# Layer 2's weights times the adjacency, on GpSimd and in the adjacency's own tile

## The chip, the cores and the metric

The kernel runs on one core of a Trainium2 chip. A core has five engines with instruction queues of their own: TensorE (PE in the profile; PEld are its weight loads), VectorE (DVE), ScalarE (ACT), GpSimd (POOL) and SyncE (SP), which issues the DMAs here. Each engine works through its queue in order; semaphores order the engines among each other. The metric is the device time of one execution in microseconds (us). Lower is better.

## The reference

Four layers over a batch of 32 graphs, each with 512 nodes, 64 features and a weighted 512x512 adjacency. Each layer adds its result to x and normalises.

```python
x = layernorm(x + L0(x, adj))            # (adj / clip(deg, 1)) @ x
x = layernorm(x + L1(x, adj, W, b))      # Chebyshev polynomials of the Laplacian, k = 4
x = layernorm(x + L2(x, adj, attW, attb))
x = layernorm(x + L3(x, adj, mask, W1, b1, W2, b2))

# layer 2
x_local = logmap(x[:, :, None, :], x[:, None, :, :], c)    # all pairs i, j
logits  = concat([x_self, x_local]) @ att_W + att_b
att     = sigmoid(logits) * adj
support = einsum('bij,bijd->bid', att, x_local)
out     = proj(expmap(clip(support), x, c), c)

# layer 3: neighbours are the places with adj > 0 without the diagonal; where a node has
# more than 10, some are removed; then a weighted sum of the 0.25, 0.5 and 0.75 quantiles
# of the neighbours' features goes through a two-layer perceptron
```

The change touches layer 2's product with `adj`, and what layer 3 reads of `adj`.

## The kernel before

All work of all 32 graphs is written down first and issued afterwards. Each helper (`tt`, `ts`, `stt`, `act`, `mm`, `tr`, `gtt`, `gts`) calls `Order.op` with the engine, a planned issue time, a planned tail, a closure, and the tiles that it writes and reads. `Order.op` finds the dependencies in program order: read after write, write after read, and the turn of a tile's buffers. `Order.issue` then simulates the five engines with the planned times, picks on each the ready operation with the earliest due time, and issues all of them in that order, pinned on each engine. A due time is 80 us times the graph's number plus a place in its lane's stage (`STAGES`, L1420). On PE it puts filler matmuls (L1458) into planned idle time. The planned cost of a DVE `tt` on two f32 tiles in SBUF is 0.07 us + 1.04 ns per element.

The lanes of a graph, in the order in which they are written down:

- `front` (due -0.6 to -0.5): four column blocks of the adjacency are loaded into `A`, transposed on PE and copied by ACT into `AT` (L780), a tile of [128, 4, 512] f32 with two buffers. Layers 0 and 1 multiply by it. The result goes into `FL`.
- `pairs` (due 1.2 to 1.3): layer 2 over all pairs of nodes, with tiles of one buffer each (`FT`, `EX`, `RW`, `Q`, `L`, `Wt`). `Q` holds a factor of the logarithmic map for each pair; its upper blocks come from a `tt` on DVE (L1066), the lower ones from transposes of these and an ACT copy. `L` is the sigmoid of the logits, made from a matmul in PSUM times `Q` (L1076). Then `Q` is multiplied by `AT` (L1080), `L` is transposed and multiplied by this product into `Wt` (L1086), and `Wt` goes through matmuls with `FL`.
- `tail` (due 0.2 to 1.5): the rest of layer 2, many small [128, 4] operations on POOL and wider ones on DVE; it ends with `x3` and `x3h`.
- `graph` (due 0.9 to 1.0): layer 3's neighbours. `nbT` is the comparison `AT > 0` on DVE (L787), with the diagonal taken out. From it come degrees, the removed edges `v`, the mask `V`, the order of nodes by degree, `perm`, `VP` and `slot`.
- `gather` (2.7 to 2.9): one-hot tiles `oh` from `slot` on DVE, matmuls with `x3h`, ACT copies into `SB` and `SH`.
- `sort` and `head` (4.5 to 5.6): sorting networks of `tt` minima and maxima on DVE over `SB` and `SH`, products with tables, layer 3's perceptron and the output.

The lanes of several graphs are interleaved on every engine. In the profile a tile's name has its lane in front: `pairs_Q`, `front_AT`, `graph_nbT`. Lines are often those of a helper: L448 is `tt`, L452 `ts`, L455 `stt`, L471 `gtt`, L475 `gts`, L483 `act`, L502 `mm`, L507 `tr`, L719 the power on POOL in `rsqrt`.

In program order, `pairs` of a graph is written down before its `graph`. Before the change `graph` and the product of L1080 only read `AT`, so they wait for nothing of each other.

Of the kernel before, what the change touches and what calls it, by code (L numbers as in the profile page):

```python
# [15 lines left out]
OP = mybir.AluOpType  # L16
# [387 lines left out]
def tile_adj_resnorm(ctx: ExitStack, tc: tile.TileContext, x, adj, nodemask, w1k, b1k, att_w, att_b,  # L404
                     w1, b1, w2, b2, out):
    nc = tc.nc
    B, N, D = x.shape
    T = N // P
# [16 lines left out]
    seq = Order(nc, tc)  # L425
# [7 lines left out]
    def vec(f, out, ins, one=False, scalars=(), reads=None, **kw):  # L433

        n = width(reads if reads is not None else out)
        tiles = [out] + list(ins)
        rate = 1.04e-3
        if not any(a.space == PSUM for a in tiles):
            half = all(a.dtype in (F16, BF16) for a in tiles)
            if one:  # L440
                rate = 0.26e-3 if half else 0.52e-3
            elif half:
                rate = 0.52e-3
        sc = [a for a in scalars if isinstance(a, bass.AP)]
        seq.op("DVE", 0.07 + n * rate + 0.065 * len(sc), 0.085, f, [out], list(ins) + sc)

    def tt(out, a, b, op):
        vec(lambda: nc.vector.tensor_tensor(out, a, b, op=op), out, [a, b])  # L448
# [5 lines left out]
    def stt(out, a, s, b, op0, op1):  # L454
        vec(lambda: nc.vector.scalar_tensor_tensor(out, a, s, b, op0=op0, op1=op1), out, [a, b], False, (s,))  # L455
# [21 lines left out]
    def act(out, a, f, bias=None, scale=1.0, accum_out=None, after=None):  # L477
        sc = [x for x in (bias, scale) if isinstance(x, bass.AP)]
        kw = {k: v for k, v in (("bias", bias), ("accum_out", accum_out)) if v is not None}
        n = width(out)  # L480
        table = "exp" if f in (AF.Ln, AF.Exp) else "sig" if f in (AF.Sigmoid, AF.Tanh) else None
        seq.op("ACT", 0.12 + n * 0.83e-3 + 0.09 * len(sc) + (0.2 if accum_out is not None else 0.0),
             0.3, lambda: nc.scalar.activation(out, a, f, scale=scale, **kw), [out, accum_out], [a, after] + sc, table)  # L483
# [22 lines left out]
    def tr(out, a, ident):  # L506
        seq.op("PE", 0.115 if a.dtype == F32 else 0.058, 0.6, lambda: nc.tensor.transpose(out, a, ident), [out], [a, ident],  # L507
               (128, 64 if width(a) <= 64 else 128))
# [6 lines left out]
    def bank(dtype=F32, home=None):  # L515
        lane, seq.lane = seq.lane, home or seq.lane
        t = seq.tile(pools["ps"], [P, 512 if dtype == F32 else 1024], dtype, "bank", bufs=BANKS.get(seq.lane, 2))
        seq.lane = lane
        return t
# [219 lines left out]
    def rowsum(a, b, name):  # L739

        pr = wide("pr")
        tt(pr, a, b, op=OP.mult)
        s = col(name)
        reduce(s, pr, OP.add)
        return s
# [223 lines left out]
    def pairs(b, res):  # L969

        mid = pools["mid"]
        AT, FL = res["AT"], res["FL"]
# [3 lines left out]
        pt = bank()  # L976
# [51 lines left out]
        pt = bank()  # L1028
# [9 lines left out]
        for j in range(T):  # L1038
            n = N - j * P
            o = slice(OB[j], OB[j + 1])  # L1040
            pt = bank()
            mm(pt[:, :n], FT[:D + 3, 2, j * P:(j + 1) * P], FT[:D + 3, 0, j * P:], start=True, stop=True)
            act(E[:, o], pt[:, :n], AF.Relu)
            pt = bank()
# [16 lines left out]
        Q = seq.tile(mid, [P, T, N], F32, "Q", 1)  # L1061
        for o in parts2:
            tt(W[:, o], W[:, o], X[:, o], op=OP.subtract)
        for j in range(T):
            o = slice(OB[j], OB[j + 1])
            tt(Q[:, j, j * P:], R[:, o], W[:, o], op=OP.mult)  # L1066
            if j:
                pt = bank()
# [4 lines left out]
        for i in range(T):  # L1073
            pt = bank()
            mm(pt, FT[:D + 3, 1, i * P:(i + 1) * P], FT[:D + 3, 2, :], start=True, stop=True)
            stt(L[:, i, :], pt, 0.5, Q[:, i, :], op0=OP.mult, op1=OP.mult)  # L1076
            act(L[:, i, :], L[:, i, :], AF.Sigmoid, bias=oo[:, i:i + 1])
        for g in range(2):
            gs = slice(2 * g, 2 * g + 2)
            tt(Q[:, gs, :], Q[:, gs, :], AT[:, gs, :], op=OP.mult)  # L1080
        Wt = seq.tile(mid, [P, T, N], F32, "Wt", 1, "RW")
        for j in range(T):
            pt = bank()
            for i in range(T):
                tr(pt[:, i * P:(i + 1) * P], L[:, i, j * P:(j + 1) * P], identf)
            stt(Wt[:, j, :], pt, 0.5, Q[:, j, :], op0=OP.mult, op1=OP.mult)  # L1086
        pt = bank()[:, :T * (D + 2)].rearrange("p (t n) -> p t n", n=D + 2)
        for t in range(T):
            for j in range(T):
# [8 lines left out]
        q = rowsum(x2, S, "xs")  # L1098
# [325 lines left out]
    with ExitStack() as fast:  # L1424
# [42 lines left out]
        for b in range(B):  # L1467
            if b % 2 == 0:
                both = {"ends": []}
            res = dict(both)  # L1470
            seq.batch = b
            for lane, f in (("front", front), ("pairs", pairs), ("graph", stage_graph), ("gather", gather), ("sort", sort)):
                seq.lane = lane
                f(b, res)
            both["ends"].append((res["slots"][1], res["x3"][0]))
            both.update(ohm=res["ohm"], ap=res["ap"])
            if b == B - 1:
                both["spots"] = spots(both["ends"])
            if b % 2:
                seq.lane = "head"  # L1480
                head(b, both)
# [144 lines left out]
    with tc.If(flagv > 0):  # L1626
        with ExitStack() as slow:
# [31 lines left out]
            for h in range(2):  # L1659
                f = cst.tile([P, D], F32, name=f"fold{h}")  # L1660
                g = cst.tile([P, D], F32, name="foldg")
# [48 lines left out]
```

## Time and profile before

| what | us |
|---|---|
| median of three runs (lowest to highest) | 2580.22 (2572.68 to 2582.51) |
| the profiled execution's own time | 2575.55 |
| its span, from the first to the last instruction | 2573.7 |
| DVE busy, of the span | 2382.1 |
| PE busy, of which L1458's filler matmuls 141.5 | 2413.6 |
| ACT busy | 1837.6 |
| POOL busy | 848.9 |
| DVE: the product of `Q` and `AT`, 64 of [128, 1024] | 78.2 |
| DVE: the comparison into `nbT`, 32 of [128, 2048] | 38.9 |

Busy time is the union of an engine's instructions; "mean ns" of a row is the length of one record, and neighbouring records of DVE overlap at their ends. The granted TensorE clock was 0.979 over the span. The four busiest rows of DVE are the two sorting networks (SB 566.8 us, SH 341.6 us), the one-hots (257.0 us) and a product of layer 2 (103.6 us). POOL's largest rows are the powers of `rsqrt` on [128, 4], some 1.2 to 1.3 us each; its products on [128, 4] have a mean of 0.25 to 0.5 us.

### The profile page before, as it was taken

Reading aid. Unit: us, or ns where it says so; the run is one execution under the profiler, and the core shown is the slowest. Engines: PE = TensorE matmul, PEld = TensorE weight load, DVE = VectorE, ACT = ScalarE, POOL = GpSimd, SP = SyncE. Lnnn points to the kernel's source line nnn. Section 1 sums busy time; section 2 is a strip of 40 time slices with the busy share of each in tenths; the row PEclk is TensorE's granted clock in tenths of the full one; section 3 lists DMA queues with packets and bytes.
Section 4 is the critical chain, followed back from the end, with each engine's and each line's share of the span. In section 5 each row is a group of like instructions: output and inputs, shape, how many; then the busy total and the mean of one; then the engine's idle time right before and its main releaser. Section 6 shows DMA issues by size and latency. Waiting matters only on the chain.

```text
span 2573.7 us, 56084 instructions
## 1 busy us (share of the span) xinstructions
PE 2413.6 (94%) x19895; PEld 1635.0 (64%) x19918; DVE 2382.1 (93%) x8937; ACT 1837.6 (71%) x4156; POOL 848.9 (33%) x2007
## 2 busy tenths in 40 slices
PE   7999989999999999999999999999999999999997
PEld 6766666656666666666666666666666666666555
DVE  4669999999999999999999999999999999999996
ACT  5766677777677777777677776877777777777761
POOL 1234434333234333323343433333333333333210
PEclk9999999999899999999999999998999999999998
DMA  1100000000000000000000000000000000000000
GB/s 39 36 22 21 22 14 13 24 22 26 20 15 19 16 26 22 24 10 22 22 20 26 22 22 22 12 22 20 26 22 18 16 18 24 20 12 3 8 5 8
DMA packets 119723, 49.98 MB, mean 19 GB/s; under 512 B 53740, under 2 KB 119436, under 8 KB 119436
## 3 DMA queue, kind: packets, MB, share of 16 engines
q1 hardware_dynamic: 118272, 46.15, 6.5%
q8 instruction: 158, 2.59, 0.4%
q14 instruction: 129, 1.06, 0.1%
q10 hardware_dynamic: 1164, 0.18, 0.0%
HBM read 37.93 MB, written 8.39 MB: 18 GB/s over the span
## 4 chain that ended last, share of the span: by engine, by line
DVE 73%; PE 20%; ACT 4%; issue 2%; POOL 1%; DMA 0%; ACTq 0%; DVEq 0%
DVE SB L448 17%; DVE SH L448 10%; DVE gather_oh L452 7%; PE pairs_bank L502 4%; DVE pairs_Q L448 4%; PE front_bank L502 4%; PE graph_bank L502 3%; PE gather_bank L502 3%; DVE pairs_RW L448 3%; DVE sort_prod L448 3%; DVE pairs_Wt L455 3%; DVE pairs_L L455 2%; PE head_bank L502 2%; DVE pairs_RW L455 2%; DVE pairs_EX L448 1%
## 5 line engine op out<-in xcount | busy, mean ns | idle before, releaser
L448 DVE TENSOR_TENSOR SB<-SB 128x92 f32<-128x92 f32 (+11 forms) x1424 | 566.8, 425 | 12.6
L502 PE MATMUL gather_bank<-gather_oh,tail_x3h 128*64 128x448 f16 (+5 forms) x5376 | 522.0, 319 | 5.6 <-ACT SB L483 4.2
L502 PEld LDWEIGHTS <-tail_x3h 128*64 128x64 bf16 x5376 | 294.7, 110 | 201.8 <-issue 95.7
L448 DVE TENSOR_TENSOR SH<-SH 128x128 f32<-128x128 f32 (+10 forms) x1744 | 341.6, 247 | 7.8
L502 PE MATMUL pairs_bank<-pairs_FT 67*128 67x512 f32 (+7 forms) x768 | 323.0, 522 | 16.6 <-DVE pairs_EX L455 9.4
L452 DVE TENSOR_SCALAR gather_oh<-graph_slot 128x256 f16<-128x256 f16 (+9 forms) x864 | 257.0, 337 | 19.1 <-PE gather_bank L502 17.0
L502 PE MATMUL front_bank<-front_AT,front_y 128*64 128x256 f32 x1536 | 193.5, 387 | 16.5 <-DVE front_y L448 15.5
L502 PEld LDWEIGHTS pairs_bank<-pairs_FT 67*128 67x128 f32 (+1 forms) x768 | 132.3, 196 | 85.3 <-issue 22.7
L502 PEld LDWEIGHTS front_bank<-front_AT,front_y 128*64 128x64 f32 x1536 | 118.1, 138 | 72.7 <-DVE front_y L448 18.9
L502 PE MATMUL graph_bank<-graph_perm,graph_V 128*128 128x512 f16 x512 | 141.6, 384 | 17.4 <-DVE graph_perm L452 16.0
L502 PEld LDWEIGHTS <-graph_nbT 128*128 128x128 f16 x1536 | 113.2, 99 | 57.7 <-issue 15.3
L1458 PE MATMUL PA<-zero 128*128 128x256 bf16 x1022 | 141.5, 280 | 0.1
L502 PEld LDWEIGHTS front_bank<-XA,front_AT 128*128 128x128 f32 x1024 | 126.2, 192 | 15.7 <-issue 6.6
L471 POOL TENSOR_TENSOR tail_nr<-tail_nr,tail_y 128x4 f32<-128x4 f32 x96 | 37.1, 386 | 285.6 <-DVE tail_y L461 230.4
L719 POOL TENSOR_TENSOR front_rs<-front_var,mhalf 128x4 f32<-128x4 f32 x64 | 81.5, 1273 | 145.7 <-DVE front_var L452 130.1
L502 PE MATMUL pairs_bank<-FLS,pairs_Wt 128*128 128x66 f32 x1024 | 123.8, 275 | 2.7 <-DVE pairs_Wt L455 2.2
L502 PEld LDWEIGHTS pairs_bank<-FLS,pairs_Wt 128*128 128x128 f32 x1024 | 119.4, 192 | 9.1 <-DVE pairs_Wt L455 7.1
L502 PE MATMUL front_bank<-XA,front_AT 128*128 128x65 f32 x1024 | 124.4, 272 | 0.3 <-ACT front_AT L483 0.3
L502 PEld LDWEIGHTS <-tabs 128*128 128x128 f16 x1296 | 78.6, 98 | 62.4 <-issue 49.6
L448 DVE TENSOR_TENSOR pairs_RW<-pairs_RW,pairs_EX 128x640 f32<-128x640 f32 x128 | 103.6, 816 | 13.7 <-ACT pairs_RW L483 9.2
L1458 PEld LDWEIGHTS <-zero 128*128 128x128 bf16 x1022 | 98.9, 101 | 23.8 <-issue 8.5
L483 ACT ACTIVATE SB<-gather_bank 128x448 f32<-128x448 f32 (+2 forms) x192 | 80.9, 439 | 45.0 <-PE gather_bank L502 44.2
(355 smaller groups left out, 6451.8 us busy)
## 6 DMA issues: line engine op xcount, KB each, us to landing
front_A<-in_adj_dram SPq DMA_DIRECT2D x128, 256.0 KB, 2.7
XA<-in_x_dram SPq DMA_DIRECT2D x32, 128.0 KB, 2.3
xs<-tail_x SPq DMA_DIRECT2D x32, 128.0 KB, 1.9
out_dram<-head_zo SPq DMA_DIRECT2D x31, 128.0 KB, 2.0
out_dram<-tail_ends SPq DMA_DIRECT2D x1, 128.0 KB, 2.1
wk<-in_L_gnn_weight_dram ACTq DMA_DIRECT2D x1, 64.0 KB, 3.1
w1s<-in_L_gnn_W_dram ACTq DMA_DIRECT2D x2, 32.0 KB, 1.9
attw<-in_L_gnn_att_W_dram ACTq DMA_DIRECT2D x2, 0.2 KB, 3.5
```

Of the source, the lines that this page charges most:

```text
L448: vec(lambda: nc.vector.tensor_tensor(out, a, b, op=op), out, [a, b])
L452: vec(lambda: nc.vector.tensor_scalar(out, a, s1, s2, op0=op0, **kw), out, [a], True, (s1, s2))
L455: vec(lambda: nc.vector.scalar_tensor_tensor(out, a, s, b, op0=op0, op1=op1), out, [a, b], False, (s,))
L471: gp(lambda: nc.gpsimd.tensor_tensor(out, a, b, op=op), out, [a, b])
L483: 0.3, lambda: nc.scalar.activation(out, a, f, scale=scale, **kw), [out, accum_out], [a, after] + sc, table)
L502: return nc.tensor.matmul(out, w, a, start=start, stop=stop)
L719: seq.op("POOL", 0.8, 0.6, lambda: nc.gpsimd.tensor_tensor(y, v, mhalf, op=OP.pow), [y], [v])
L1458: return nc.tensor.matmul(PA[:, 2 * P:], zero[:, :P], zero, start=False, stop=False)
```

## The change

The two DVE products of 1024 elements per partition become four POOL products of 512 elements, one for each row block. Each multiplies a row block of `AT` by the row block of `Q` and writes the result over that row block of `AT`. `Wt` is made from `AT` in place of `Q`. The planner is told 1.2 us for a product and a tail of 0.5 us.

```diff
-        for g in range(2):
-            gs = slice(2 * g, 2 * g + 2)
-            tt(Q[:, gs, :], Q[:, gs, :], AT[:, gs, :], op=OP.mult)
+        for j in range(T):
+            a = AT[:, j, :]
+            seq.op("POOL", 1.2, 0.5, lambda a=a, q=Q[:, j, :]: nc.gpsimd.tensor_tensor(a, a, q, op=OP.mult), [a], [a, Q[:, j, :]])
         Wt = seq.tile(mid, [P, T, N], F32, "Wt", 1, "RW")
         for j in range(T):
             pt = bank()
             for i in range(T):
                 tr(pt[:, i * P:(i + 1) * P], L[:, i, j * P:(j + 1) * P], identf)
-            stt(Wt[:, j, :], pt, 0.5, Q[:, j, :], op0=OP.mult, op1=OP.mult)
+            stt(Wt[:, j, :], pt, 0.5, AT[:, j, :], op0=OP.mult, op1=OP.mult)
```

Three relations change with it. The product no longer writes `Q`, so it does not wait until the four `L` have read `Q`. `AT` is written in `pairs`, so `graph`'s comparison, which comes later in program order, now waits for the product and reads it in place of the adjacency; off the diagonal the factor in `Q` is positive, so the comparison with zero means the same. And `AT` is read until the last `Wt` is made.

## The prediction

> **What bounds the kernel now.** I read the page's first lines, then the slices and the chain of waits.
>
> ```profile
> PE 2413.6 (94%) x19895; PEld 1635.0 (64%) x19918; DVE 2382.1 (93%) x8937; ACT 1837.6 (71%) x4156; POOL 848.9 (33%) x2007
> ...
> DVE  4669999999999999999999999999999999999996
> ...
> DVE 73%; PE 20%; ACT 4%; issue 2%; POOL 1%; DMA 0%; ACTq 0%; DVEq 0%
> ```
>
> After a start of about 190 us DVE is full to the last slice, and the chain that ended last runs over it for 73% of the span. PE looks as busy, but 141.5 us of it are the fillers of L1458, which are issued only into planned idle time; its own work is 2413.6 - 141.5 = 2272.1 us. A table of stretches gives the steady state exactly (columns: PE, PEld, DVE, ACT, POOL busy).
>
> ```profile
> core 0: us, PE busy (x) PEld busy (x) DVE busy (x) ACT busy (x) POOL busy (x), PEclk, DMA share, GB/s
> ...
> 600.00:1200.00 600.00, 570.38 (x4685) 383.34 (x4690) 577.88 (x2172) 450.32 (x1024) 199.29 (x475) 0.98 0.08 21
> 1200.00:1800.00 600.00, 569.47 (x4680) 382.63 (x4684) 576.40 (x2155) 441.44 (x1009) 210.24 (x478) 0.98 0.07 20
> 1800.00:2400.00 600.00, 567.39 (x4664) 378.44 (x4669) 581.46 (x2179) 449.96 (x1020) 212.63 (x479) 0.99 0.06 17
> ```
>
> DVE is busy 96 to 97% there. So a microsecond of DVE time given back or lost on each graph moves the end by about as much; POOL has two thirds of its time free.
>
> **What is removed.** The view of the tile Q shows the product that goes, and its two neighbours on DVE.
>
> ```profile
> L455 DVE SCALAR_TENSOR_TENSOR pairs_L<-pairs_bank,pairs_Q x128: 651/681/693, 104.0 to 2422.3; 128x512 f32<-128x512 f32 x128
> L455 DVE SCALAR_TENSOR_TENSOR pairs_Wt<-pairs_bank,pairs_Q x128: 658/680/692, 111.9 to 2430.0; 128x512 f32<-128x512 f32 x128
> L448 DVE TENSOR_TENSOR pairs_Q<-pairs_Q,front_AT x64: 1203/1224/1261, 105.6 to 2423.2; 128x1024 f32<-128x1024 f32 x64
> ```
>
> Sixty-four products of 1.224 us each (shortest, median, longest in ns). Records of DVE overlap by some 80 ns: where another follows at once, the next starts 1.14 us after. Gain: 64 x 1.14 = 73 us of DVE. The stt that makes Wt keeps its size and only reads AT in place of Q: nothing changes in its 0.68 us.
>
> **What is added.** 128 products of 128x512 f32 on POOL. No POOL instruction of the trace reads more than 8 elements per partition; its widest that write are in the start-up:
>
> ```profile
> 1.03 0.53 POOL L539 MEMSET UC<- 128x512 f16 x1
> ...
> 1.65 0.56 POOL L547 IOTA ii<- 128x512 int32 x1
> 2.16 0.14 POOL L550 IOTA ic<- 128x4 int32 x1
> ```
>
> From 4 to 512 elements iota grows by 0.42 us, 0.83 ns per element, for one stream written. A 128x4 product takes 0.20 us undisturbed. With one, two or three such streams one after the other a 128x512 product takes 0.62, 1.04 or 1.46 us. I take 1.04: two operands read, the write beside them. POOL gains 128 x 1.04 = 133 us, from 849 to 982 of some 2,600: no bound in itself.
>
> **What it does to DVE** decides the sign. One window has both cases, POOL first, DVE second:
>
> ```profile
> 1589.07 0.20 POOL L471 TENSOR_TENSOR pairs_sq<-FLS 128x4 f32<-128x4 f32 x1
> 1589.23 0.20 POOL L475 TENSOR_SCALAR pairs_two<-FLS 128x4 f32<-128x4 f32 x1
> 1589.52 1.13 POOL L471 TENSOR_TENSOR pairs_al<-pairs_two,FLS 128x4 f32<-128x4 f32 x1
> ```
>
> ```profile
> 1588.70 0.68 DVE L455 SCALAR_TENSOR_TENSOR pairs_L<-pairs_bank,pairs_Q 128x512 f32<-128x512 f32 x1
> 1589.30 0.16 DVE L452 TENSOR_SCALAR FLS<-FLS 128x8 f32<-128x8 f32 x1
> 1589.37 1.21 DVE L448 TENSOR_TENSOR pairs_Q<-pairs_Q,front_AT 128x1024 f32<-128x1024 f32 x1
> ```
>
> Under pairs_L, with one operand in PSUM, a POOL instruction of four elements takes 0.20 us. Under the product with two operands in SBUF, such an instruction takes 1.13 us and ends when that product ends. This is regular. I took all small POOL instructions that begin with over 250 ns of a DVE instruction still to go: under SB<-SB 128x448 all 92 were held until about 0.14 us after its end, under gather_oh 128x1792 all 26, under pairs_L none of 45, under pairs_Wt none of 22. So one engine at a time has the way to SBUF, for a whole DVE instruction. The reverse is not in the trace: POOL's own accesses are too short, and DVE's SB 128x448 takes 620 ns beside POOL work and 617 without it. Bounds of what a POOL product costs DVE: nothing, if DVE goes first and POOL gets the gaps; or its whole 0.62 to 1.46 us, if POOL holds as DVE does. I take that it holds, the nearest row being DVE's own holding, and POOL streams all the while.
>
> Not every DVE instruction wants the way then. Adding up DVE from 200 to 2400 us, each until the next starts, instructions with two SBUF operands or a tensor_scalar in SBUF take 1677 of 2122 us (79%); in the 15 us after the last tt into Q, where the new products fall, 10.3 of 15 us (69%). I take 75%. Cost: 128 x 1.04 x 0.75 = 100 us of DVE, with 0.62 and 1.46 as ends 60 and 140. Net on DVE: -73 + 100 = +27, from -13 to +67.
>
> The Trainium skill, "SBUF — State Buffer", section "Who interferes with whom", speaks against this change. It says that a DVE instruction with two SBUF inputs and a GpSimd one that reads SBUF exclude each other, and that whichever is issued second is blocked fully until the first is done. The trace agrees for POOL as second, with the 1.13 us above; no run here shows DVE as second. By the rule the net is the +27 just worked out, by the rows alone it could also be the -73.
>
> **What is moved.** Three things wait longer. (1) The product now lies in AT, and the graph lane's comparison (L787) reads AT later in program order, so it waits for POOL.
>
> ```profile
> L452 DVE TENSOR_SCALAR graph_nbT<-front_AT x32: 1193/1218/1229, 29.0 to 2390.3; 128x2048 f16<-128x2048 f32 x32
> ```
>
> It ran 22 to 33 us ahead of the product (batch 31: 2390.3 against 2423.2). From it to the batch's last slot copy passed 57 us in batch 0, 86 in batch 20, 74 in batch 31. Batch 20: slot would be done at 1593 + 4 + 86 = 1683 in place of 1636, 21 us after x3h (1662), which gather's matmuls need too. What hides these 21 us is the wait of sort: the last one-hot of batch 20 was made at 1722, its sorted sum was out at 1833, 111 us for a lane with 566.8/32 = 18 us of DVE work on SB. The cover ends with the run: slot(31) goes from 2465 to 2424 + 4 + 57 to 74 = 2485 to 2502, against x3h(31) at 2492, 0 to +10; I take +8, near the 74 of the same stretch. (2) AT's two buffers come free at the last Wt, in batch 20 at 1599.2, not at the product's end, 1592.8, after which the copies into AT of batch 22 began at 1593.5: 6.4 us later. The cover is the time that FL is ready before FT is copied, mostly 15 to 25 us (batch 22: 1662 to 1688). If it were gone, half of 6.4 us per graph, 102 us. I take 0. (3) Small POOL operations queue behind the products: those of tail, front's rsqrt, head's. Up to 4 x 1.04 = 4.2 us per graph; POOL is 1% of the chain, and DVE has other lanes' work meanwhile; 0, at worst 133 us in all. Wt waits for the products itself, but from the last tt into Q to the last sigmoid are some 19 us (batch 20: 1574 to 1593), against 4.2 us. No DMA is added or removed; loads into A wait, if at all, with the copies of (2).
>
> The order is laid out anew with 1.2 us for each product and 2.3 us less DVE per graph. DVE's idle share of 3 to 4% may change by a point either way: 22 us in 2,200.
>
> **Sum.** The profiled execution took 2575.6 us (span 2573.7 and 1.9 around it). 2575.6 - 73 + 100 + 8 = 2610.6. The median of the runs lies 4.6 higher, at 2580.2: 2615.
>
> **Rivals.**
> (B) DVE goes first, and POOL works in its gaps and under its PSUM instructions: 2580 - 73 + 8 = 2515, 2505 to 2545 as the order falls. For it: POOL waited through several DVE instructions on end (3.58 us from 1341.9). Against it: usually it got in after the one instruction it met. PE would not stop it: its 2272 us are below DVE's 2309. This is the case on the other side: it decides from where a POOL product costs DVE less than 73/128 = 0.57 us, or, with the 8 us, 0.51.
> (C) The hand-over of AT or POOL's queue gets on the path besides: with half of the 102 us, 2666; for it: in batches 3 and 15 FL was ready only 6 us ahead. Against it: the mean cover is twice what is added.
> (D) Gain and blocking cancel, products falling under pairs_L and pairs_Wt, which let POOL through (2.4 us each per graph): 128 x 1.04 x 0.5 = 67, so 2582.
>
> **How the numbers follow.** Forecast (A) 0.60, B 0.20, C 0.14, D 0.06. The time is A's, 2615; A's own range, with a hold of 0.62 to 1.46 us and part of the order's 22 us, is 2565 to 2665. With C's lower half and B's upper half: 2525 to 2672. Half a per cent, 13 us, is what a measurement can tell from no change: 2567 to 2593. Faster: B 0.19 and 0.03 of A, 0.22. Same: D 0.06, 0.01 of B, 0.11 of A, 0.18. Slower 0.60.
>
> **What would show it.** POOL should have 128 products into front_AT of about 1.04 us plus a wait for DVE. The blocking shows in DVE's rows: SB<-SB 128x448 with a longest far above its 620 ns, or idle time before it with no releaser, some 100 us in all. If these rows are unchanged, B is right. graph_nbT should start after the products in every batch; FL ready less than 6 us ahead of FT, batch after batch, would be C. The forecast is wrong if the POOL product is under 0.6 us or lasts several us with DVE undisturbed.

## The result and the profile after

The changed kernel takes 2760.95 us (median of 4 runs, 2752.60 to 2767.77), the kernel before 2581.36 us (median of 4) beside it: ratio 1.070, 95% interval 1.0673 to 1.0727. It is 180 us slower; 2615 us was forecast, with a range of 2565 to 2665. The page of the changed kernel, its lines of busy time, the slices of DVE and of PE's granted clock, and the chain:

```profile
span 2756.0 us, 56866 instructions
...
PE 2552.2 (93%) x20227; PEld 1704.1 (62%) x20252; DVE 2427.4 (88%) x8873; ACT 1798.2 (65%) x4126; POOL 997.3 (36%) x2135
...
DVE  3568989999899989898998989989999888998996
...
PEclk9999989988999998999999989999999999998999
...
DVE 59%; PE 35%; ACT 3%; issue 1%; POOL 1%; DMA 0%; ACTq 0%; DVEq 0%; POOLq 0%
```

DVE lost 73 us of products and is yet busy 45.3 us longer (2427.4 against 2382.1). The larger part of the loss is DVE's idle time: span less busy is 328.6 us against 191.6, 137.0 more. PE's share of the chain rose from 20% to 35%. The same in the table of stretches (PE, PEld, DVE, ACT, POOL busy, then the clock):

```profile
600.00:1200.00 600.00, 563.61 (x4395) 367.36 (x4400) 551.81 (x2028) 416.59 (x949) 230.07 (x479) 0.93 0.07 19
1200.00:1800.00 600.00, 560.23 (x4364) 368.22 (x4368) 550.13 (x1979) 404.07 (x936) 233.40 (x463) 0.93 0.07 18
1800.00:2400.00 600.00, 553.09 (x4557) 374.17 (x4565) 554.39 (x2047) 398.82 (x942) 228.81 (x481) 0.97 0.07 20
```

DVE is busy 92% of the steady state, before 96 to 97%. The first two stretches, before and after:

```profile
0.00:200.00 200.00, 181.63 (x1494) 136.49 (x1496) 111.72 (x422) 130.55 (x280) 52.62 (x209) 1.00 0.12 32
200.00:600.00 400.00, 373.39 (x3083) 251.72 (x3081) 386.21 (x1400) 281.84 (x641) 148.66 (x321) 0.97 0.07 19
```

```profile
0.00:200.00 200.00, 181.91 (x1504) 142.62 (x1505) 101.55 (x382) 112.11 (x239) 57.85 (x201) 1.00 0.11 31
200.00:600.00 400.00, 372.55 (x2867) 243.88 (x2870) 358.13 (x1264) 257.52 (x597) 151.92 (x317) 0.90 0.07 18
```

The view of the tile AT and that of nbT:

```profile
L1080 POOL TENSOR_TENSOR front_AT<-front_AT,pairs_Q x128: 1255/1334/4228, 94.9 to 2594.4; 128x512 f32<-128x512 f32 x128
...
L452 DVE TENSOR_SCALAR graph_nbT<-front_AT x32: 1185/1214/1222, 103.3 to 2602.3; 128x2048 f16<-128x2048 f32 x32
```

A product takes 1.26 us undisturbed (the shortest). The first nbT starts at 103.3 us, after the first products, and no longer at 29.0. Where products come in a row, this is what DVE does beside them. First POOL, then DVE, then PE, in the same window:

```profile
1040.71 5.21 POOL L1080 TENSOR_TENSOR front_AT<-front_AT,pairs_Q 128x512 f32<-128x512 f32 x3 [4.23 <-ACT pairs_Q L483]
```

```profile
1042.15 0.20 DVE L448 TENSOR_TENSOR SB<-SB 128x52 f32<-128x52 f32 x1
1042.27 1.28 DVE L448 TENSOR_TENSOR PRS<-PRS 128x64 f32<-128x64 f32 x1
1043.48 1.28 DVE L448 TENSOR_TENSOR SB<-SB 128x52 f32<-128x52 f32 x1
1044.69 1.31 DVE L448 TENSOR_TENSOR PRS<-PRS 128x64 f32<-128x64 f32 x1
1045.92 1.45 DVE L448 TENSOR_TENSOR SB<-SB 128x52 f32<-128x52 f32 x3
```

```profile
1042.59 0.38 PE L502 MATMUL PA<-zero 128*128 128x512 bf16 x1
1046.05 0.64 PE L502 MATMUL head_bank<-identf,PRS 128*32 128x128 f32 x2 [3.08 <-DVE PRS L448]
```

The 5.21 us of POOL are three products: the first waited for DVE until 1042.2 and so lasted 2.77 us, the next two 1.26 us each. A DVE instruction of 52 elements needs 0.20 us. From 1042.27 each waits for a whole product: DVE gets one instruction through per product, 1.2 us apart. The last row is three instructions merged, after the products. PE has a matmul at the head of its queue that needs the last PRS and sits idle for 3.08 us. TensorE's granted clock (the number after the five busy times) falls in the second of these three stretches:

```profile
1020.00:1040.00 20.00, 19.11 (x176) 11.70 (x173) 17.77 (x48) 13.74 (x30) 6.50 (x11) 1.00 0.00 1
1040.00:1064.00 24.00, 20.59 (x103) 13.00 (x100) 20.11 (x71) 12.23 (x26) 12.56 (x17) 0.64 0.03 6
1064.00:1100.00 36.00, 35.63 (x297) 23.74 (x296) 35.19 (x124) 26.48 (x64) 13.02 (x34) 1.00 0.12 34
```

The granted clock is 0.64 over the 24 us, which the clock's own records give as 0.5 from 1045.85 to 1062.92 and 1 elsewhere; the drop comes 2.9 us after PE's gap began at 1042.97. "Half-clock time" below is the sum of such stretches of a run: 111 us before, 326 us after. PE's gaps of over 2 us, added up from the trace, are 2 with 6 us before, 19 with 55 us after, 14 of these beside a product. Two numbers more are added up from the trace for each kernel: the stretch of DVE (the sum by which its records are longer than the mean of their form before; 113 us after), and DVE's idle time (span less busy).

### The profile page after: what moved, and what is told of

Same layout as the page of the kernel before. It is cut to its first block, busy times and chain, and to the rows that moved or that the text cites. A ratio compares the mean times of both kernels' runs of the same rounds, so it can differ in the third digit from the quotient of the medians.

```text
span 2756.0 us, 56866 instructions
## 1 busy us (share of the span) xinstructions
PE 2552.2 (93%) x20227; PEld 1704.1 (62%) x20252; DVE 2427.4 (88%) x8873; ACT 1798.2 (65%) x4126; POOL 997.3 (36%) x2135
## 4 chain that ended last, share of the span: by engine, by line
DVE 59%; PE 35%; ACT 3%; issue 1%; POOL 1%; DMA 0%; ACTq 0%; DVEq 0%; POOLq 0%
DVE SB L448 15%; DVE SH L448 8%; DVE gather_oh L452 7%; PE pairs_bank L502 7%; PE front_bank L502 6%; PE gather_bank L502 6%; PE graph_bank L502 5%; PE head_bank L502 3%; PE PA L1458 3%; DVE pairs_RW L448 3%; DVE sort_prod L448 2%; DVE pairs_Wt L455 2%; PE pairs_bank L507 2%; PE front_bank L507 1%; DVE pairs_Q L448 1%
## 5 line engine op out<-in xcount | busy, mean ns | idle before, releaser
L448 DVE TENSOR_TENSOR SB<-SB 128x448 f32<-128x448 f32 (+11 forms) x1424 | 593.8, 443 | 13.9 <-ACT SB L483 3.2
L502 PE MATMUL gather_bank<-gather_oh,tail_x3h 128*64 128x448 f16 (+5 forms) x5376 | 533.6, 324 | 0.7 <-ACT SB L483 0.7
L502 PE MATMUL pairs_bank<-pairs_FT 67*128 67x512 f32 (+7 forms) x768 | 352.0, 566 | 21.9 <-DVE pairs_L L455 19.8
L448 DVE TENSOR_TENSOR SH<-SH 128x128 f32<-128x128 f32 (+11 forms) x1744 | 347.7, 250 | 8.5
L452 DVE TENSOR_SCALAR gather_oh<-graph_slot 128x256 f16<-128x256 f16 (+9 forms) x864 | 288.6, 378 | 34.7 <-PE gather_bank L502 30.2
L1080 POOL TENSOR_TENSOR front_AT<-front_AT,pairs_Q 128x512 f32<-128x512 f32 x128 | 196.0, 1537 | 141.6 <-DVE pairs_Q L448 84.3
L1458 PE MATMUL PA<-zero 128*128 128x256 bf16 x1325 | 186.9, 286 | 0.5 <-issue 0.2
L1458 PEld LDWEIGHTS <-zero 128*128 128x128 bf16 x1325 | 132.9, 103 | 40.4 <-issue 18.8
L483 ACT ACTIVATE graph_v<-graph_bank,graph_c 128x512 f16<-128x512 f32 x128 | 87.8, 686 | 92.0 <-PE graph_bank L502 84.9
L483 ACT ACTIVATE graph_VP<-graph_bank 128x512 f16<-128x512 f32 x128 | 75.4, 589 | 75.3 <-PE graph_bank L502 60.9
```

What stands on the lines that cost most here:

```text
L452: vec(lambda: nc.vector.tensor_scalar(out, a, s1, s2, op0=op0, **kw), out, [a], True, (s1, s2))
L502: return nc.tensor.matmul(out, w, a, start=start, stop=stop)
L1080: seq.op("POOL", 1.2, 0.5, lambda a=a, q=Q[:, j, :]: nc.gpsimd.tensor_tensor(a, a, q, op=OP.mult), [a], [a, Q[:, j, :]])
L1458: return nc.tensor.matmul(PA[:, 2 * P:], zero[:, :P], zero, start=False, stop=False)
```

## The experiments

Each was timed beside the kernel before on the same chip; times are medians, and what is read from a trace belongs to the one profiled execution. Of each edit the lines that carry it are shown.

**POOL or the order.** The change does two things: POOL holds DVE up, and graph and AT's release wait. These four take them apart.

POOL's products write Q, graph reads the untouched AT:

```diff
-            tt(Q[:, gs, :], Q[:, gs, :], AT[:, gs, :], op=OP.mult)
+            a = Q[:, j, :]
+            seq.op("POOL", 1.2, 0.5, lambda a=a, q=AT[:, j, :]: nc.gpsimd.tensor_tensor(a, a, q, op=OP.mult), [a], [a, AT[:, j, :]])
```

> The four POOL products write Q, as the DVE products did, so graph reads the untouched AT and waits for nothing of pairs. Theory port (POOL's products block DVE, the order costs little): almost the whole loss stays, 2720 to 2770 us. Theory order (graph's wait for the products and the later release of AT cost most of the 180 us, the blocking only its net of some 45 us of DVE): 2600 to 2650 us, DVE's SB 128x448 still with a longest of about 1.7 us, PE's granted clock back at 0.97 or more.

2666.3 against 2582.3 us, ratio 1.034 (1.0309 to 1.0372): between the two theories. Stretch 100 us, half-clock time 154, DVE idle 247. Of the 180 us some 96 are gone, though the products are as many and as long.

The DVE products write AT:

```diff
-            tt(Q[:, gs, :], Q[:, gs, :], AT[:, gs, :], op=OP.mult)
+            tt(AT[:, gs, :], AT[:, gs, :], Q[:, gs, :], op=OP.mult)
...
-            stt(Wt[:, j, :], pt, 0.5, Q[:, j, :], op0=OP.mult, op1=OP.mult)
+            stt(Wt[:, j, :], pt, 0.5, AT[:, j, :], op0=OP.mult, op1=OP.mult)
```

> The two DVE products are kept but write AT, and Wt reads AT: the changed order of graph without any POOL product. Theory port: 2570 to 2600 us, as before. Theory order: 2660 to 2730 us, granted clock near 0.94, DVE's rows without stretched instructions, DVE idle 7 to 8% in the steady state.

2635.2 against 2582.3 us, 1.021 (1.0177 to 1.0236), again between the two theories: the order costs 53 us by itself, and not by the clock (half-clock time 113 us, stretch 1 us, DVE idle 248 us). It is paid early: the copies into AT of graph 8 begin at 574 us against 525, 49 us late; those of graph 24 at 1810 against 1755, 55 us late.

The changed kernel with graph written ahead of pairs:

```diff
-            for lane, f in (("front", front), ("pairs", pairs), ("graph", stage_graph), ("gather", gather), ("sort", sort)):
+            for lane, f in (("front", front), ("graph", stage_graph), ("pairs", pairs), ("gather", gather), ("sort", sort)):
```

> The changed kernel with graph written down ahead of pairs, so that graph's comparison reads AT before the POOL products overwrite it; AT is still held until the last Wt. Theory port: 2720 to 2770 us. Theory order, if graph's wait is what counts: 2600 to 2650 us as for POOL into Q; if the later release of AT is what counts: above 2700 us.

2732.3 against 2582.3 us, 1.058 (1.0547 to 1.0621), 29 us less than the changed kernel: graph's wait is not what makes the changed kernel so much slower than POOL into Q. Left over were AT's later release and the products' place: here 121 of 128 start before the first L of their graph, as in the changed kernel 122, and with POOL into Q none, since writing Q must wait until L has read it.

Four spare POOL products beside the kernel before (each reads 128 columns of Q four times over, after the DVE product, as both operands, and writes a tile in f16 that nothing reads):

```diff
+        for j in range(T):
+            d = seq.tile(pools["small"], [P, T, P], F16, "spare", 1)
+            i4 = Q[:, j, :P].unsqueeze(1).to_broadcast([P, T, P])
+            seq.op("POOL", 1.2, 0.5, lambda d=d, i4=i4: nc.gpsimd.tensor_tensor(d, i4, i4, op=OP.mult), [d], [Q[:, j, :P]])
```

> The kernel before with four spare POOL products of 128x512 f32 per graph beside it, read from Q after the DVE product and written to a tile that nothing reads: the blocking by itself, with nothing saved and nothing waiting. Theory port: the blocking alone costs 180 us and more, 2760 us or above. Theory order: DVE busy grows by 90 to 120 us and the time by as much, 2670 to 2700 us, granted clock 0.97 or more.

2709.4 against 2582.3 us, 1.051 (1.0478 to 1.0536), 127 us: above the one theory's 2700, below the other's 2760. DVE's busy time rose by 74 us, its idle time by 57. These products are shorter, 1.03 us; whether by the operands or by the output was not tried. Blocking costs more than the time that it blocks.

**AT's release, the clock, and no POOL.** POOL into Wt's tile, which is free by then; the stt works in place:

```diff
+            a = Wt[:, j, :]
+            seq.op("POOL", 1.2, 0.5, lambda a=a, b=AT[:, j, :], q=Q[:, j, :]: nc.gpsimd.tensor_tensor(a, b, q, op=OP.mult), [a], [AT[:, j, :], Q[:, j, :]])
...
-            stt(Wt[:, j, :], pt, 0.5, AT[:, j, :], op0=OP.mult, op1=OP.mult)
+            stt(Wt[:, j, :], pt, 0.5, Wt[:, j, :], op0=OP.mult, op1=OP.mult)
```

> The POOL products write Wt's tile, free by then, and the stt works on it in place: products as early and as close together as in the changed kernel, but AT is released at the products' end and graph reads the untouched AT. Theory AT (the later release of AT costs what is left between POOL into Q and graph first, 66 us): 2640 to 2675 us, half-clock time near 150 us. Theory burst (products straight after Q hold DVE for 5 us on end, PE idles and its clock halves): 2690 to 2730 us, half-clock time 250 us or more, as with graph first.

2773.2 against 2580.6 us, 1.073 (1.0714 to 1.0753). Graph reads the untouched AT and AT is released at the products' end, and yet the kernel is as slow as the changed one: the theory of AT falls. It is also 43 us above what the burst theory allowed. Half-clock time 310 us, stretch 143, PE's gaps of over 2 us 31 with 99 us.

Four more fillers at each product's planned time, in the changed kernel:

```diff
+            if e == "POOL" and ops[i][1] == 1.2:
+                for _ in range(4):
+                    before["PE"] = self.pin(filler(), before.get("PE"))
```

> The changed kernel with four more filler matmuls on PE at the planned time of each product, 16 per graph, 512 in all, some 70 us of PE. Theory burst: they keep PE from idling there, half-clock time falls from 326 to below 220 us and the time by 20 to 80 us in spite of PE's extra work. Theory AT: the clock is a by-product; half-clock time may fall, the time stays within 15 us of 2761 or rises by up to 70.

2743.9 us, ratio to before 1.062 (1.0596 to 1.0645): half-clock time falls to 199 us, as the burst theory said, the time by 17 us only, short of its 20 and just beyond the 15 of the other.

No POOL product, the DVE products into Wt's tile:

```diff
+            tt(Wt[:, gs, :], Q[:, gs, :], AT[:, gs, :], op=OP.mult)
```

> No POOL product: the two DVE products of before, into Wt's tile, so that they wait for no L and AT is released as before or sooner. Both theories: within 0.5% of before, 2565 to 2595 us, perhaps a little below, since the product may go before the last L.

2592.1 against 2580.6 us, 1.0032 (1.0016 to 1.0048): no gain from freeing the product of its wait for L. The copies into AT of graph 8 begin at 541 us here, against 525 before.

**Length of one product, and the order's two parts.**

```diff
-            a = AT[:, j, :]
-            seq.op("POOL", 1.2, 0.5, lambda a=a, q=Q[:, j, :]: nc.gpsimd.tensor_tensor(a, a, q, op=OP.mult), [a], [a, Q[:, j, :]])
+            for c in range(T):
+                a, q = AT[:, j, c * P:(c + 1) * P], Q[:, j, c * P:(c + 1) * P]
+                seq.op("POOL", 0.35, 0.5, lambda a=a, q=q: nc.gpsimd.tensor_tensor(a, a, q, op=OP.mult), [a], [a, q])
```

> The changed kernel with each product cut into four of 128x128 f32, 512 in all, planned at 0.35 us each. Theory burst (beside a run of products DVE gets one instruction through per product, so PE's wait for DVE's result grows with the length of one product): PE's gaps over 2 us become rare, half-clock time at or below 200 us from 326, time 2680 to 2730 us, although POOL works longer in all. Rival, total hold (what counts is the sum of POOL's holding): half-clock time stays near 320 us, time 2750 to 2800 us.

```diff
+        for g in range(2):
+            a, q = AT[:, 2 * g:2 * g + 2, :], Q[:, 2 * g:2 * g + 2, :]
+            seq.op("POOL", 2.4, 0.5, lambda a=a, q=q: nc.gpsimd.tensor_tensor(a, a, q, op=OP.mult), [a], [a, q])
```

> The changed kernel with two products of 128x1024 f32 per graph, planned at 2.4 us each: the same holding in half as many, twice as long pieces. Theory burst: DVE's longest records near 2.6 us, PE's gaps over 2 us more numerous than the 19 of the changed kernel, half-clock time above 326 us, time 2770 to 2830 us. Rival, total hold: 2740 to 2770 us.

Narrow: 2715.7 against 2582.6 us, 1.053 (1.0483 to 1.0584). Wide: 2788.9, 1.081 (1.0745 to 1.0877). Both times as the burst theory had them; but with narrow products half-clock time is still 297 us and PE still has 19 gaps of over 2 us, against that theory. With wide ones it is 400 us and 29 gaps. The stretch is 98 us with narrow and 129 with wide products, 113 in the changed kernel, so the total of the holding did not stay the same either. The rows of the product itself, narrow and wide, and then SB's on DVE in the kernels before, changed, narrow and wide (shortest, median, longest in ns):

```profile
L1081 POOL TENSOR_TENSOR front_AT<-front_AT,pairs_Q x512: 446/465/2785, 95.0 to 2557.1; 128x128 f32<-128x128 f32 x171
```

```profile
L1080 POOL TENSOR_TENSOR front_AT<-front_AT,pairs_Q x64: 2343/2470/5833, 97.5 to 2625.0; 128x1024 f32<-128x1024 f32 x64
```

```profile
L448 DVE TENSOR_TENSOR SB<-SB x1424: 169/297/1124, 216.3 to 2536.0; 128x448 f32<-128x448 f32 x45, 128x92 f32<-128x92 f32 x43, 128x52 f32<-128x52 f32 x29, 128x132 f32<-128x132 f32 x16
```

```profile
L448 DVE TENSOR_TENSOR SB<-SB x1424: 176/316/2162, 230.0 to 2718.8; 128x448 f32<-128x448 f32 x44, 128x52 f32<-128x52 f32 x38, 128x92 f32<-128x92 f32 x35, 128x132 f32<-128x132 f32 x16
```

```profile
L448 DVE TENSOR_TENSOR SB<-SB x1424: 175/320/1360, 226.9 to 2676.3; 128x448 f32<-128x448 f32 x42, 128x92 f32<-128x92 f32 x42, 128x52 f32<-128x52 f32 x33, 128x132 f32<-128x132 f32 x16
```

```profile
L448 DVE TENSOR_TENSOR SB<-SB x1424: 170/309/3251, 223.4 to 2750.9; 128x448 f32<-128x448 f32 x44, 128x92 f32<-128x92 f32 x37, 128x52 f32<-128x52 f32 x35, 128x132 f32<-128x132 f32 x16
```

The longest grows from 1124 ns by 1038 with products of 1255 ns, by 236 with 446, by 2127 with 2343: in each case by some 0.2 us less than one product. Of the records with 52 elements the longest are 243, 1283, 479 and 2357 ns. DVE waits for one whole POOL instruction and then gets its turn.

The DVE products into AT, with graph ahead of pairs:

> The DVE products into AT, with graph written down ahead of pairs: AT is still held until the last Wt, but graph's comparison reads it first and waits for nothing. If the 53 us of DVE into AT come from AT's later hand-over to the next front, they stay: 2620 to 2645 us, and the copies into AT of graph 8 begin near 574 us. If they come from graph's wait, the time falls to 2575 to 2600 us, graph 8 near 525 us.

2599.7 against 2582.6 us, 1.0085 (1.0057 to 1.0113), the copies of graph 8 at 541 us. Of the 53 us of DVE into AT, 35 are graph's wait; 17 stay with AT's later release and the lanes written in another order, which were not separated. DVE into Wt has neither wait, and its copies of graph 8 begin at 541 us too, so part of the 17 may be no more than a new order.

**Place or plan.** POOL into Wt's tile, each product after the L of its row block (the planner sees the wait as with Q, and a real dependency on that stt is added):

```diff
+                tc.add_manual_dep(r.ins, made[j].name, mybir.DependencyInfo(mybir.DependencyClass.Sync, mybir.DependencyReason.DATA), reason="after L")
```

> POOL into Wt's tile once more, but each product waits until DVE has made the L of its row block, as it had to where it wrote Q. Theory early (products that start straight after Q hold DVE just when PE waits for its results, and the same products later cost less): 2640 to 2690 us as with POOL into Q, half-clock time 130 to 200 us. Rival, that POOL into Wt is slow for another reason (its place in the plan, the tile): 2740 to 2780 us, half-clock time 300 us.

2658.7 against 2584.5 us, 1.031 (1.028 to 1.034); half-clock time 148 us, PE's gaps of over 2 us 15 with 41 us. The same products into the same tile cost 114 us less when they start after L. The stretch is 109 us against 143, DVE's idle time 241 us against 314: they hold DVE less, and the engines wait less for each other.

The kernel before without fillers:

```diff
-                for _ in range(int((t - spare - fill) / 0.11)):
+                for _ in range(0):
```

> The kernel before without its filler matmuls: PE idles more and the clock halves more often, with no POOL product and no changed order. It prices half-clock time. If half-clock time is what the changed kernel's added 215 us of it cost most of its 137 us of DVE idling: half-clock time of 300 us and more, and the time up by 0.3 to 0.6 us per added us of it, 2640 us or above at 300. If the clock is a by-product: the time stays below 2600 us whatever the clock.

2599.3 against 2584.5 us, 1.0067 (1.0047 to 1.0088), with half-clock time at 266 us. 155 us more of it cost 15 us, about 0.1 us each; the case of 0.3 to 0.6 us is out. The run with more fillers gives nearly the same (127 us less half-clock time, 17 us). For the 215 us that the change added this makes an estimate of some 25 us. It is a low one: the first run also takes PE work away, the second adds some, and both would hide part of the price. DVE into AT, though, has 56 us more DVE idle time than before at an unchanged half-clock time, so the engines can wait for each other without the clock. PE's slower clock is mostly a by-product, as far as these runs go.

Then the order itself was tried. `Order.issue` fixes the order on every engine from planned times, in which DVE is never held. The planner is told of 0.9 us of DVE for each product, with no instruction behind it, in the changed kernel and in POOL into Wt:

```diff
+            if fn is None:
+                continue
...
+            seq.op("DVE", 0.9, 0.0, None, [], [Q[:, j, :]])
```

> The changed kernel, and its planner is told of 0.9 us of DVE time for each product, with no instruction behind it (the 113 us by which DVE's records grew, over 128 products). Theory plan (the order on every engine is fixed ahead for a DVE that is not held, so that 5 us of holding before the first L leaves PE and DVE waiting for each other): DVE's idle time falls from 329 us to 290 or less and the time to 2700 us or below, with DVE's records as long as before. Rival, place (products before the first L hold what is urgent whatever the plan): 2740 to 2790 us.

> POOL into Wt's tile with products straight after Q, and the same 0.9 us of planned DVE time for each. Theory plan: from 2773 us to 2710 us or below, towards the 2659 us of the same products after L. Rival, place: 2740 us or above.

The changed kernel goes from 2761 to 2680.5 us (1.038 to before, 1.0356 to 1.0411), POOL into Wt from 2773 to 2665.4 us (1.033, 1.0299 to 1.0353). DVE's busy time in the first, 2425.3 us, is that of the changed kernel, 2427.4:

```profile
PE 2516.8 (93%) x20288; PEld 1678.1 (62%) x20316; DVE 2425.3 (90%) x8873; ACT 1806.4 (67%) x4132; POOL 1004.1 (37%) x2135
```

Stretch is 119 us there (113 unplanned), DVE idle 271 us (329), half-clock time 190 us, PE's gaps of over 2 us 6 with 14 us. The profiled execution is the slowest of five, 2697.9 us, so these figures show 60 of the 80 us. Its stretches:

```profile
0.00:200.00 200.00, 183.09 (x1483) 142.78 (x1485) 100.10 (x367) 109.93 (x236) 56.61 (x199) 0.98 0.11 30
200.00:600.00 400.00, 369.65 (x2961) 246.22 (x2962) 357.87 (x1256) 255.20 (x593) 146.11 (x318) 0.95 0.07 19
600.00:1200.00 600.00, 565.79 (x4591) 369.46 (x4599) 580.46 (x2124) 431.80 (x987) 245.27 (x492) 0.98 0.07 19
1200.00:1800.00 600.00, 566.88 (x4532) 374.22 (x4537) 565.70 (x2098) 422.03 (x979) 245.19 (x492) 0.96 0.07 20
1800.00:2400.00 600.00, 565.43 (x4498) 369.30 (x4503) 557.73 (x2005) 421.90 (x958) 235.08 (x475) 0.96 0.07 18
```

In the first 600 us DVE idles 142 us, as in the changed kernel (140; before 102). After them it idles 129 us against 188 (before 90): what went is there. POOL and DVE hold each other as long as in the changed kernel, and the products have not moved behind L: 117 of 128 still start before the first L of their graph (122 unplanned). So what went is the waiting of the engines for each other. POOL into Wt keeps its place too (107 of 128, 117 unplanned), but there some 35 of its 108 us are shorter holding, stretch 108 us against 143. The place costs little once it is planned for: POOL into Wt before L, planned, is within 7 us of the same after L. A told time in a kernel whose DVE nothing holds was not tried, so some of the gain may be any new order's; the one new order without POOL products, AT's later release or graph's wait, DVE into Wt, differs from the kernel before by under 12 us. No version with POOL products came near the kernel before.

## Why the prediction was wrong

**The bound** was read rightly: DVE was full, and what it lost moved the end.

**Removed and added.** The 73 us went. A product takes 1.26 us, inside 0.62 to 1.46, above the 1.04 chosen, and 1.54 us on average with its waits for DVE.

**POOL holds as DVE does** was right. The stretch is 113 us against the 100 of the sum, 0.88 us per product, and DVE's net is +45.3 us against +27. The term was a little small, and the sign was right: a product saves DVE 73/128 = 0.57 us. One reading was off without harm: a small POOL instruction held under SB 128x448 ended 0.06 us after it (median of the 92), not 0.14. The rule of the Trainium skill, "SBUF — State Buffer", section "Who interferes with whom", that the one issued second is blocked fully, is now shown for DVE as second too: a record of 0.20 us becomes 1.28 us beside a product of 1.26.

**The step that failed** is "The order is laid out anew ... DVE's idle share of 3 to 4% may change by a point either way: 22 us in 2,200." I priced the new plan as if its times stayed true. They did not: the plan gives DVE 2.3 us less per graph, and the chip holds it 3.5 us more (113/32). With the order pinned on every engine, a late DVE result stops PE at the head of its queue (the 3.08 us above), and later DVE waits for PE: its idle time before `front_st`, which PE's matmuls release, went from 16.0 to 45.9 us. DVE's idle time rose by 137 us, six times the 22 allowed; telling the planner of the stall takes 80 us off the changed kernel and 108 off POOL into Wt.

**What is moved** was the second miss. For graph's wait I took 8 us, from batches 20 and 31, where it is covered; by DVE into AT, with graph after and ahead, it costs 35 us, and it costs most of them in the first eight graphs (with graph ahead the copies of graph 8 begin 33 us sooner, and DVE idles 105 us of the first 600 in place of 131), which I did not price. There DVE was not full (111.7 of the first 200 us), and early graph work filled it. I also misread how far the comparison ran ahead of the product: not 22 to 33 us but 28 to 87, and 77 to 87 in the first four graphs, so the wait is longest where I did not look. For AT's release I took 0; it is at most 17 us. POOL's queue was not tried by itself.

**The sum.** 45 (DVE's net), 80 (the unplanned stall), 35 and up to 17 (graph, AT) make 177 of 180 us, and that they come so close is partly luck, since they do not simply add: putting graph ahead took only 29 us off the changed kernel, POOL into Wt has neither of the two waits and was slower still, and the two better versions of it (after L, or planned) keep 49 to 55 us of added DVE idle time that was not traced further. That cause stays open.

**The rivals.** B fell: DVE does wait. D fell. C was right that something comes besides, but named AT's hand-over or POOL's queue, and its 2666 us is 95 us short.

## What to carry to other kernels

An elementwise instruction on GpSimd that reads SBUF is largely paid for by VectorE where VectorE works on two SBUF operands (here 0.88 of a product's 1.26 us on average, 1.08 in the window shown): compare that, not zero, with what VectorE saves. Where an order is fixed ahead from modelled times, an engine that holds up another has to be in the model; the error is paid not once but at every engine that then waits in the wrong order. And a dependency that is covered in the steady state is priced in the start-up too, where the engine that bounds is not yet full.

## What the runs showed of the hardware

- VectorE and GpSimd take turns by whole instructions: beside a run of products DVE, on two SBUF operands, got one instruction through per product, 1.2 us apart.
- A product on GpSimd takes 0.45, 1.26 and 2.34 us for 128, 512 and 1024 elements of f32, 2.1 ns per element; with 128 elements read four times over as both operands and an f16 output 1.03 us for 512.
- In the changed kernel each of the 18 gaps of over 2 us on PE after the first 12 us (2.06 to 5.29 us) was followed, 1.8 to 5.0 us after it began, by 3.4 to 20.5 us at a granted clock of 0.5; of the 41 gaps of 1 to 2 us 14 were, within 5.1 us. In this kernel a us of half clock cost about 0.1 us, at the low estimate above.
